# Expert rows weighted at their eviction, and gathers that add into the tokens' rows, in a two-layer Mamba/attention/mixture-of-experts kernel

## Chip, core and metric

The kernel runs on one core of a Trainium2 chip. The metric is the device time of one execution in microseconds (us). Engines are named as in the profile: PE (TensorE), DVE (VectorE), ACT (ScalarE), POOL (GpSimd), SP (SyncE, which here only issues DMAs). Each engine runs its own instructions strictly in order; they meet at semaphores. Indirect DMAs (gather and scatter by a list of row numbers) are issued by POOL and make up the software queue q0; SP's DMAs are q1 and ACT's q10.

## What is computed

Two layers over 8 x 512 tokens of 256 features. Layer 0 adds a bidirectional state-space block and a top-1 mixture of experts. Layer 1 adds attention over a low-rank latent and a top-2 mixture with a capacity. The change touches only that last mixture:

```python
cap = ceil(n_tok / n_exp * 1.0)                     # 4096 / 8 = 512
weights_flat = softmax(x @ router_w.T + router_b)   # [4096, 8]
topk_vals, topk_idx = top_k(weights_flat, 2)        # expert 7 is a no-op
sorted_indices = argsort(-expert_mask, axis=0)[:cap]    # the first 512 tokens of each expert
inputs = x_flat[used_idx] * sorted_mask
h = relu(einsum('ceh,ehi->cei', inputs, experts_inter))
out = einsum('cei,eih->ceh', h, experts_out) * in_w[..., None]
combined = zeros.at[used_idx].add(out)
combined = combined + x_flat * (noop_w * noop_mask)[:, None]
```

Each of seven experts takes the first 512 tokens that chose it; later choices of it are dropped. Choice 8 is a no-op that adds the token's own normalised row times its share. Each token thus gets back at most two expert rows, each times the softmax share of that expert.

## The kernel before

The 4096 tokens are 32 blocks of 128 (`NTILE`), four to a batch of 512. All of layer 1's second half runs under an order written out by hand (`manual_schedule`), so that the order of the Python calls is the order on every engine.

The frame is attention: 128 steps (8 batches x 4 groups of heads x 4 query blocks, loop at L1504 and after), each for four heads. PE makes scores (L1379), DVE evicts them with a clamp (L1384) and multiplies by the decay band taking the row maximum (L1386), ACT takes exponentials (L1394), PE transposes (L1401), ACT evicts these (L1402), PE multiplies by the values (L1410). A step is `now.scores()`, then slots of other work with `fill()`, then the later parts of the two steps before. In a slot, `fill()` takes the next piece of urgent work (projections of the next batch, the output projection `finish`) or, when there is none, of the experts. Only when both are empty does `more()` advance the combine by one turn, so a step has two combine turns once the experts are done.

- **Routing**, `route1` (L1154): softmax `pr` over the experts, the two choices as one-hot masks, ranks by a prefix sum over tokens, slots. `slot1[:, i, k]` is the row of the expert's buffer that holds choice k of the tokens in block i; dropped and no-op choices get row `NSLOT1`. `wsel[k]` holds the shares of choice k (L1201).
- **Send**, `send_rows` (L1286): per block, two scatters on POOL (L1296) send the block's rows to their slots in `xd1` (DRAM), where a row number beyond the buffer is dropped; then DVE adds the no-op part to `x_sb` (L1303), which holds the residual rows of all tokens in SBUF. `ask_rows` loads four blocks ahead. `turn` (L1313) copies the two columns of row numbers of a block to a small tile `at`, of which there are six, since each DMA needs a list of its own.
- **Experts**, `experts` (L1217): for each of seven experts and two halves of 256 slots: load rows (`expert_rows`), transpose, two matmuls with a relu between, evict the result with an ACT copy (L1254), store to `yd1` in DRAM (L1256).
- **Combine**, `combine` (L1337): a turn per block makes two gathers on POOL (L1344) from `yd1` into tiles `yg` of their own, 14 of them; six turns later `add` (L1355) does two weighted adds on DVE (L1358), `x_sb += yg[k] * wsel[k]`. After every fourth block the batch is marked as combined, and if its `finish` has run, `send` (L1333) stores it with SP (L1335). Row `NSLOT1` of `yd1` is zeroed, so dropped choices add zero.
- **Finish** (L1319) of a batch: output projection on PE, eviction on ACT, add to `x_sb` on DVE (L1327).

Of the kernel before, what the change touches and what calls it, by code (L numbers as in the profile page):

```python
# [9 lines left out]
FP = mybir.dt.float32  # L10
# [26 lines left out]
NE1 = NE - 1  # L37
NSLOT1 = NE1 * CAP
HALF = CAP // 2


AH, AD, DL = 16, 16, 64
# [15 lines left out]
def tile_kernel(ctx: ExitStack, tc: tile.TileContext, t, out: bass.AP):  # L58
# [6 lines left out]
    def ctile(name, shape, dtype=FP, pool=None):  # L65
        return (pool or const).tile(shape, dtype, name=name, tag=name)
# [27 lines left out]
    G.iota(iota_t, pattern=[[P, NTILE]], base=0, channel_multiplier=0, allow_small_or_imprecise_dtypes=True)  # L94
    iota_b = ctile("iota_b", [P, NBLK])
    G.iota(iota_b, pattern=[[1, NBLK]], base=0, channel_multiplier=0, allow_small_or_imprecise_dtypes=True)
    zero = ctile("zero", [P, DM])
    G.memset(zero, 0.0)


    xd0 = dram.tile([NBLK * P, DM], FP, name="xd0", tag="xd0")
    yd0 = dram.tile([NBLK * P, DM], FP, name="yd0", tag="yd0")
    xd1 = dram.tile([NSLOT1, DM], FP, name="xd1", tag="xd1")
    yd1 = dram.tile([NSLOT1 + 1, DM], FP, name="yd1", tag="yd1")

    x1 = dram.tile([NT, DM], FP, name="x1", tag="x1")
# [11 lines left out]
    def clear(dst, rows, lo, hi):  # L118

        n = rows // P  # L120
        A.dma_start(
            out=dst[: n * P, :].rearrange("(p r) d -> p r d", p=P)[:, lo:hi, :], in_=bc(zero, 1, [P, hi - lo, DM])
        )


# [353 lines left out]
        Y.dma_start(out=exd.rearrange("g p l -> p g l"), in_=e8)  # L479

    steps()
    l1c = tl = w_r = rb = w_q = w_o = w_uk = w_uv = w_kv = band = slot1 = wsel = proj1 = vt0 = qk0 = r1b = noop = None
    tls = ExitStack()
    for k in range(HC):
        V.tensor_scalar(w_out[:, k, :], w_out[:, k, :], norm_w[:, k : k + 1], None, ALU.mult)
# [1 line left out]
    with ExitStack() as es:  # L487
# [168 lines left out]

        def second_weights():

            nonlocal l1c, tl, w_r, rb, w_q, w_o, w_uk, w_uv, w_kv, band, slot1, wsel, proj1, vt0, qk0
            es.close()  # L660
            l1c = ctx.enter_context(tc.tile_pool(name="l1c", bufs=1, side="right"))
            tl = tls.enter_context(tc.tile_pool(name="tl", bufs=1, side="right"))
            w_r = load("w_r", [P, KC, NE], l1c)
            rb = load("rb", [P, NE], l1c)
            w_q = load("w_q", [P, KC, DM], l1c)
            w_o = load("w_o", [P, KC, DM], l1c)
            w_uk = load("w_uk", [DL, DM], l1c)

            w_uv = ctile("w_uv", [DL + 1, VW], pool=l1c)
            G.memset(w_uv, 0.0)  # L670
            hv = w_uv[:, : AH * (AD + 1)].rearrange("p (h e) -> p h e", e=AD + 1)
            Y.dma_start(out=hv[:DL, :, :AD], in_=t["w_uv"])
            G.memset(hv[DL : DL + 1, :, AD : AD + 1], 1.0)
            slot1 = ctile("slot1", [P, NTILE, 2], I32, l1c)
            wsel = [l1c.tile([P, NTILE], FP, name=f"wsel{k}", tag=f"wsel{k}") for k in range(2)]
            proj1 = ctile("proj1", [P, NTILE, NE], pool=l1c)
            vt0 = ctile("vt0", [P, TPB, VW], pool=l1c)
            qk0 = rows_qk()

            band = ctile("band", [P, NBAND], pool=l1c)  # L680
            G.iota(
                band, pattern=[[1, NBAND]], base=P - S, channel_multiplier=-1, allow_small_or_imprecise_dtypes=True
            )

            w_kv = ctile("w_kv", [P, KC, DL], pool=l1c)
            both = tl.tile([P, 2, KC, DM], FP, name="w_kt", tag="xr", bufs=2)
            Y.dma_start(out=both[:, 0], in_=t["w_kt"])
# [15 lines left out]
            V.tensor_copy(w_kv, wp)  # L703
            yield
# [330 lines left out]
        with tc.manual_schedule(engines=ENGINES):  # L1035
# [39 lines left out]
            for n in range(N):  # L1075
# [43 lines left out]
                if n % 8 == 3 and n // 8 < NE1:  # L1119
                    e = n // 8  # L1120
                    clear(xd1, NSLOT1, TPB * e, TPB * (e + 1))
                    if e == 0:
                        A.dma_start(out=yd1[NSLOT1 : NSLOT1 + 1, :], in_=zero[0:1, :])
            last = batch[B - 1]
            pending.append(last.gate())
            while pending:
# [17 lines left out]
    with tc.tile_pool(name="a1", bufs=1) as p1, tc.tile_pool(name="a2", bufs=2) as p2, tc.tile_pool(  # L1144
# [9 lines left out]
        def route1():  # L1154
# [29 lines left out]


            V.tensor_tensor(noop, pr[:, :, NE1], mask[:, :, NE1], ALU.mult)


            valid = big.tile(E3, FP, name="valid", tag="valid")
# [5 lines left out]
            for k, (m, oh) in enumerate(((m1, oh1), (m2, oh2))):  # L1195
                yield
                V.tensor_tensor(oh, oh, valid, ALU.mult)
                sl = slots_of(big, oh, rank, "k")
                V.tensor_scalar(sl, sl, float(NSLOT1), None, ALU.add)
                V.tensor_copy(slot1[:, :, k], sl)  # L1200
                V.tensor_copy(wsel[k], slots_of(big, oh, pr, "w"))  # L1201

        def expert_rows(e, half):
            at = slice(e * CAP + half * HALF, e * CAP + (half + 1) * HALF)
            xd = e2.tile([P, 2, DM], FP, name="e_xd", tag="e_rows")
            Y.dma_start(out=xd, in_=xd1[at, :].rearrange("(c p) d -> p c d", p=P))
            return xd  # L1210

# [5 lines left out]
        def experts():  # L1217
            w1, xd = expert_w1(0), expert_rows(0, 0)
            yield
            for e in range(NE1):  # L1220
                w2 = e1.tile([P, FC, DM], FP, name="e_w2", tag="e_w2")
                Y.dma_start(out=w2, in_=t["eo"][e])
                for half in range(2):
# [3 lines left out]
                    for k in range(KC):  # L1227
                        for c in range(2):
                            T.transpose(tp[:, k, c * P : (c + 1) * P], xd[:, c, k * P : (k + 1) * P], ident)
                    A.copy(xdT, tp)  # L1230
                    yield
                    hT = e1.tile([P, FC, HALF], FP, name="e_hT", tag="e_hT")
                    for f in range(FC):
# [8 lines left out]
                        xd = expert_rows(e, 1)  # L1242
                    elif e + 1 < NE1:
                        w1, xd = expert_w1(e + 1), expert_rows(e + 1, 0)
                    yo = e2.tile([P, 2, DM], FP, name="e_yo", tag="e_rows")
                    for c in range(2):
                        yp = bank("e_yp", [P, DM])
                        for f in range(FC):
                            T.matmul(  # L1249
                                yp, hT[:, f, c * P : (c + 1) * P], w2[:, f, :], start=(f == 0), stop=(f == FC - 1)  # L1250
                            )
                            if f % 2 == 1 and f < FC - 1:
                                yield True
                        A.copy(yo[:, c, :], yp)  # L1254
                        yield
                    Y.dma_start(out=yd1[at, :].rearrange("(c p) d -> p c d", p=P), in_=yo)  # L1256

        def spread(rows, got, n, by=None):

# [26 lines left out]
        def send_rows():  # L1286

            sent = []
            for i in range(NTILE):
                b, c = i // TPB, i % TPB  # L1290
                if c == 0 and b + 2 < B:
                    ask_rows(b + 2)
                x = to_send[b][:, c, :]
                at = turn(r1b, i)
                for k in range(2):
                    one = G.indirect_dma_start(  # L1296
                        out=xd1, out_offset=bass.IndirectOffsetOnAxis(ap=at[:, k : k + 1], axis=0),
# [5 lines left out]
                V.scalar_tensor_tensor(x_sb[:, i, :], x, noop[:, i : i + 1], x_sb[:, i, :], ALU.mult, ALU.add)  # L1303
                yield

        to_send = {}

        def ask_rows(b):
            to_send[b] = r1b.tile([P, TPB, DM], FP, name="xs", tag="xs", bufs=B)
            Y.dma_start(out=to_send[b], in_=rows_of(xn1, b))  # L1310
            Y.dma_start(out=x_sb[:, b * TPB : (b + 1) * TPB, :], in_=rows_of(x1, b))

        def turn(pool, i):  # L1313

            at = pool.tile([P, 2], I32, name="at", tag="at", bufs=6)
            V.tensor_copy(at, slot1[:, i, :])
            return at

        def finish(b, oT):  # L1319
            for c in range(TPB):  # L1320
# [15 lines left out]

        def combine():  # L1337

            held = []
            for i in range(NTILE):  # L1340
                held.append((i, [e2.tile([P, DM], FP, name="yg1", tag="row1", bufs=14) for _ in range(2)]))
                at = turn(e2, i)
                for k in range(2):
                    G.indirect_dma_start(  # L1344
                        out=held[-1][1][k], out_offset=None, in_=yd1,
                        in_offset=bass.IndirectOffsetOnAxis(ap=at[:, k : k + 1], axis=0),
                        bounds_check=NSLOT1, oob_is_err=False,
                    )
                yield
                if len(held) > 6:  # L1350
                    add(*held.pop(0))
            for one in held:
                add(*one)

        def add(i, yg):  # L1355
            xi = x_sb[:, i, :]
            for k in range(2):
                V.scalar_tensor_tensor(xi, yg[k], wsel[k][:, i : i + 1], xi, ALU.mult, ALU.add)  # L1358
            b = i // TPB
            if i % TPB == TPB - 1:  # L1360
                combined.add(b)
                if b in finished:
                    send(b)

# [282 lines left out]
```

## Time and profile before

| | us |
|---|---|
| Time, median of 3 runs (lowest to highest) | 2100.1 (2098.34 to 2104.96) |
| The profiled execution | 2129.08 |
| Its span | 2127.2 |
| PE, DVE, ACT, POOL busy | 1861.6, 1461.2, 1179.0, 643.6 |
| Index copies of the send, first and last start | 1190.4 and about 1318 |
| Experts' second matmuls, first and last start | 1351.1 and 1965.4 |
| Gathers of the combine, first and last start | 1969.6 and 2091.3 |
| 64 gathers of the combine, POOL time of one (median) | 1.009 |
| 64 weighted adds, DVE time of one (median) | 0.483 |
| 28 evictions of expert rows, ACT time of one (median) | 0.373 |

An execution under the profiler is longer than the runs that are timed; the profile's durations are compared with its own 2129.08 us. In the profile a line of a timeline gives start, duration, engine, source line, operation, output and inputs, and in brackets how long the engine was idle before and what released it. Merged entries (`x2`) give the time from the first start to the last end; DVE instructions overlap[...], so the distance of two starts is what an instruction costs in a full queue. A row of the view by stretch gives, for a window in us from the start, the busy time of each engine with its number of instructions, the clock granted to TensorE (1.00 is full), the busy share of the 16 DMA engines, and GB/s. In a DMA queue's row stand packets, MB and the share of the 16 engines' time in the window.

### The profile page before, as it was taken

What the parts mean: (1) busy time and instruction counts of PE and PEld (TensorE: products, weight loads), DVE (VectorE), ACT (ScalarE), POOL (GpSimd) and SP (SyncE); (2) the same over time, 40 slices, a digit from 0 to 9 for tenths busy, and PEclk for the clock granted to TensorE, in tenths of its full rate; (3) what the DMA queues carried; (4) which work ended last, traced back from release to release, by engine and by line L of the source; (5) the groups of instructions that cost most, each with busy time, mean ns of one, the idle gap of its engine ahead of it and who ended that gap; (6) DMA issues with size and microseconds to landing.
All of it is one profiled execution on the core that took longest, in us unless ns stands there. A gap on an engine that the chain in (4) does not pass through costs nothing. (4 is left out here: it accounts for less than half of the span.)

```text
span 2127.2 us, 33330 instructions
## 1 busy us (share of the span) xinstructions
PE 1861.6 (88%) x11672; PEld 1231.4 (58%) x11672; DVE 1461.2 (69%) x3329; ACT 1179.0 (55%) x2545; POOL 643.6 (30%) x592
## 2 busy tenths in 40 slices
PE   5666999999999999986758788999999999999785
PEld 5333776767677677644535444656666666666443
DVE  5684757575575757687648886666666676767795
ACT  2243544445354544545327566777677777777663
POOL 0048645456464646345400353000000000000552
PEclk9877999999999999997858778999999999999787
DMA  7113745556555556435433342121221212221355
GB/s 259 58 55 128 239 154 190 182 170 208 169 199 181 179 172 193 126 110 158 142 96 110 104 136 76 65 96 61 66 80 62 97 59 87 65 74 56 95 108 95
DMA packets 156632, 263.67 MB, mean 124 GB/s; under 512 B 24906, under 2 KB 113022, under 8 KB 144562
## 3 DMA queue, kind: packets, MB, share of 16 engines
q1 hardware_dynamic: 124816, 144.70, 21.6%
q0 software_dynamic: 22320, 107.55, 16.4%
q10 hardware_dynamic: 9330, 9.31, 1.3%
q8 instruction: 92, 1.51, 0.3%
q14 instruction: 74, 0.61, 0.1%
HBM read 193.44 MB, written 72.75 MB: 125 GB/s over the span
## 5 line engine op out<-in xcount | busy, mean ns | idle before, releaser
L1384 DVE TENSOR_SCALAR s<-s_ps 128x512 f32<-128x512 f32 x512 | 317.8, 683 | 241.6 <-PE s_ps L1379 195.9
L1394 ACT ACTIVATE s<-s,ng 128x512 f32<-128x512 f32 x512 | 354.4, 727 | 32.8 <-DVE ng L1390 23.1
L1401 PE MATMUL p_ps<-ident,s 128*128 128x128 f32 x2048 | 301.5, 292 | 72.4 <-ACT pT L1402 61.6
L1401 PEld LDWEIGHTS p_ps<-ident,s 128*128 128x128 f32 x2048 | 247.6, 149 | 159.7 <-ACT pT L1402 91.4
L1402 ACT COPY pT<-p_ps 128x512 f32<-128x512 f32 x512 | 279.1, 590 | 91.0 <-PE p_ps L1401 63.3
L1386 DVE CUSTOM_DVE_ANT_0 s<-s,band 128x512 f32<-128x512 f32 x512 | 322.8, 688 | 0.0
L1344 POOL DMA_INDIRECT yg<-yd,at x64 | 68.3, 1067 | 705.1 <-ACT s L1394 650.4
L728 PE MATMUL pj<-xT,w_in 128*128 128x512 f32 x384 | 204.5, 660 | 16.0 <-DVE cv L741 14.2
L1379 PE MATMUL s_ps<-kT,qT 16*128 16x512 f32 x1024 | 174.1, 694 | 17.9 <-DVE s L1384 11.5
L541 PEld LDWEIGHTS h_ps<-xdT,w 128*128 128x128 f32 x1248 | 150.1, 193 | 21.0 <-issue 20.2
L541 PE MATMUL h_ps<-xdT,w 128*128 128x128 f32 x1248 | 153.7, 277 | 1.6 <-DMA w<-in_w_dram,w_idx 1.6
L741 DVE SCALAR_TENSOR_TENSOR cv<-pj,w_conv_w,cv 128x511 f32<-128x511 f32 (+2 forms) x192 | 143.1, 746 | 9.6 <-ACT cv L737 5.6
L559 PE MATMUL y_ps<-w,hT 128*128 128x256 f32 x624 | 147.4, 380 | 0.0
L904 POOL TENSOR_TENSOR au<-da,half 128x512 f32<-128x512 f32 x64 | 77.7, 1214 | 212.0 <-PE seg L920 108.1
L1410 PE MATMUL o_ps<-pT,vt 128*32 128x256 f32 x2048 | 139.0, 414 | 0.0
L559 PEld LDWEIGHTS y_ps<-w,hT 128*128 128x128 f32 x624 | 116.0, 191 | 32.1 <-issue 17.9
L728 PEld LDWEIGHTS pj<-xT,w_in 128*128 128x128 f32 x384 | 71.8, 205 | 100.3 <-issue 92.2
L978 POOL TENSOR_TENSOR yT<-yT,ex 128x512 f32<-128x512 f32 (+1 forms) x48 | 59.7, 1243 | 226.3 <-DVE ex L977 168.1
L1236 PE MATMUL e_hp<-e_xdT,e_w 128*128 128x256 f32 x448 | 121.7, 394 | 3.0 <-ACT e_xdT L1230 2.1
L1249 PE MATMUL e_yp<-e_w,e_hT 128*128 128x256 f32 x448 | 120.0, 390 | 0.2
L933 ACT ACTIVATE mt<-seg,mid 64x64 f32<-64x64 f32 x512 | 109.9, 310 | 0.8
L1410 PEld LDWEIGHTS o_ps<-pT,vt 128*32 128x32 f32 x2048 | 64.7, 117 | 77.5 <-issue 48.0
(275 smaller groups left out, 3028.8 us busy)
## 6 DMA issues: line engine op xcount, KB each, us to landing
ex<-exd SPq DMA_DIRECT2D x96, 128.0 KB
u<-in_u_dram SPq DMA_DIRECT2D x16, 512.0 KB
xtd<-xT SPq DMA_DIRECT2D x16, 512.0 KB
fr<-fdd SPq DMA_DIRECT2D x64, 128.0 KB
od<-os SPq DMA_DIRECT2D x32, 256.0 KB
xT<-xtd SPq DMA_DIRECT2D x15, 512.0 KB
e_w<-in_ei_dram SPq DMA_DIRECT2D x7, 1024.0 KB
e_w<-in_eo_dram SPq DMA_DIRECT2D x7, 1024.0 KB
```

The lines of the kernel that those rows point to most:

```text
L541: T.matmul(hp[:, i, :], w1[:, k * FF + f * P : k * FF + (f + 1) * P], xdT[:, k * P : (k + 1) * P], start=(k == 0), stop=(k == KC - 1),)
L559: T.matmul(yp, hT[f // 4][:, f % 4, :], w2[:, f * DM : (f + 1) * DM], start=(f == 0), stop=(f == FC - 1))
L728: T.matmul(pj, w_in[:, k, o * P : (o + 1) * P], self.xT[:, k, :], start=(k == 0), stop=(k == KC - 1))
L741: V.scalar_tensor_tensor(cv[:, s:], pj[:, : S - s], conv_w[:, q, 3 - s : 4 - s], cv[:, s:], ALU.mult, ALU.add)
L1236: T.matmul(hp, w1[:, k, f * P : (f + 1) * P], xdT[:, k, :], start=(k == 0), stop=(k == KC - 1))
L1379: T.matmul(sp[i], self.q[r, cols], self.k[r, :], start=True, stop=True)
L1384: V.tensor_scalar(self.p[i], sp[i], -CLAMP, CLAMP, ALU.max, ALU.min)
L1386: V.tensor_tensor_reduce(out=self.p[i], in0=self.p[i], in1=band[:, at : at + S], scale=1.0, scalar=-3.0e38, op0=ALU.mult, op1=ALU.max, acc ...
L1394: A.activation(self.p[i], self.p[i], AF.Exp, bias=self.ng[:, i : i + 1])
L1401: T.transpose(pp[:, k, :], self.p[i][:, k * P : (k + 1) * P], ident)
L1402: A.copy(pT[i][:, :, cc * P : (cc + 1) * P], pp)
L1410: T.matmul(op[32 * i : 32 * i + 32, half * 2 * P : (half + 1) * 2 * P], self.v[:, k, h * (AD + 1) : h * (AD + 1) + 32], pT[i][:, k, :], st ...
```

## The change

The row that is sent to an expert becomes 264 wide instead of 256: the block's eight shares travel behind its features. When a batch's first block is sent, DVE copies the shares of its four blocks behind the rows. The expert's loads have the wider rows, DVE copies the expert's own column of shares to a tile, and ACT multiplies by it as it evicts. `yd1` then holds weighted rows. The selection of shares in routing goes (`wsel`).

The gathers of the combine write to no tile of their own: they add in the DMA (`compute_op=ALU.add`) to the token's row in `x_sb`. A block's second gather comes three turns after its first, so the loop has 35 turns. Each gather has an index tile of its own (one column is copied), out of the same six. The weighted adds on DVE and their 14 tiles are gone, and a batch's stores are issued once the second gather of its last block has been.

```diff
+DW = DM + NE
-    zero = ctile("zero", [P, DM])
+    zero = ctile("zero", [P, DW])
-    xd1 = dram.tile([NSLOT1, DM], FP, name="xd1", tag="xd1")
+    xd1 = dram.tile([NSLOT1, DW], FP, name="xd1", tag="xd1")
...
+            to_send["shares"] = pr
...
-                V.tensor_copy(wsel[k], slots_of(big, oh, pr, "w"))
...
-            xd = e2.tile([P, 2, DM], FP, name="e_xd", tag="e_rows")
+            xd = e2.tile([P, 2, DW], FP, name="e_xd", tag="e_rows")
...
+                    share = e2.tile([P, 2], FP, name="e_sh", tag="e_sh")
+                    V.tensor_copy(share, xd[:, :, DM + e])
...
-                        A.copy(yo[:, c, :], yp)
+                        A.mul(yo[:, c, :DM], yp, share[:, c : c + 1])
...
+                if c == 0:
+                    V.tensor_copy(to_send[b][:, :, DM:], to_send["shares"][:, i : i + TPB, :])
...
-        def turn(pool, i):
-
+        def turn(pool, i, of):
+
+            of = of if isinstance(of, slice) else slice(of, of + 1)
             at = pool.tile([P, 2], I32, name="at", tag="at", bufs=6)
-            V.tensor_copy(at, slot1[:, i, :])
-            return at
+            V.tensor_copy(at[:, of], slot1[:, i, of])
+            return at[:, of]
...
         def combine():
-            held = []
-            for i in range(NTILE):
-                held.append((i, [e2.tile([P, DM], FP, name="yg1", tag="row1", bufs=14) for _ in range(2)]))
-                at = turn(e2, i)
-                for k in range(2):
-                    G.indirect_dma_start(
-                        out=held[-1][1][k], out_offset=None, in_=yd1,
-                        in_offset=bass.IndirectOffsetOnAxis(ap=at[:, k : k + 1], axis=0),
-                        bounds_check=NSLOT1, oob_is_err=False,
-                    )
+            for i in range(NTILE + 3):
+                for k, j in ((0, i), (1, i - 3)):
+                    if 0 <= j < NTILE:
+                        at = turn(e2, j, k)
+                        G.indirect_dma_start(
+                            out=x_sb[:, j, :], out_offset=None, in_=yd1,
+                            in_offset=bass.IndirectOffsetOnAxis(ap=at, axis=0),
+                            bounds_check=NSLOT1, oob_is_err=True, compute_op=ALU.add,
+                        )
+                b = j // TPB
+                if j >= 0 and j % TPB == TPB - 1:
+                    combined.add(b)
+                    if b in finished:
+                        send(b)
                 yield
-                if len(held) > 6:
-                    add(*held.pop(0))
-            for one in held:
-                add(*one)
-
-        def add(i, yg):
-            xi = x_sb[:, i, :]
-            for k in range(2):
-                V.scalar_tensor_tensor(xi, yg[k], wsel[k][:, i : i + 1], xi, ALU.mult, ALU.add)
-            ...
```

More of the change, by code (lines that the diff above doesn't have):

```diff
@@ L121, in clear @@
         A.dma_start(
-            out=dst[: n * P, :].rearrange("(p r) d -> p r d", p=P)[:, lo:hi, :], in_=bc(zero, 1, [P, hi - lo, DM])
+            out=dst[: n * P, :].rearrange("(p r) d -> p r d", p=P)[:, lo:hi, :],
+            in_=bc(zero[:, : dst.shape[1]], 1, [P, hi - lo, dst.shape[1]]),
         )
@@ L481, in tile_kernel @@
     steps()
-    l1c = tl = w_r = rb = w_q = w_o = w_uk = w_uv = w_kv = band = slot1 = wsel = proj1 = vt0 = qk0 = r1b = noop = None
+    l1c = tl = w_r = rb = w_q = w_o = w_uk = w_uv = w_kv = band = slot1 = proj1 = vt0 = qk0 = r1b = noop = None
     tls = ExitStack()
@@ L657, in second_weights @@
         def second_weights():
-            nonlocal l1c, tl, w_r, rb, w_q, w_o, w_uk, w_uv, w_kv, band, slot1, wsel, proj1, vt0, qk0
+            nonlocal l1c, tl, w_r, rb, w_q, w_o, w_uk, w_uv, w_kv, band, slot1, proj1, vt0, qk0
             es.close()
@@ L674, in second_weights @@
             slot1 = ctile("slot1", [P, NTILE, 2], I32, l1c)
-            wsel = [l1c.tile([P, NTILE], FP, name=f"wsel{k}", tag=f"wsel{k}") for k in range(2)]
             proj1 = ctile("proj1", [P, NTILE, NE], pool=l1c)
@@ L1122, in tile_kernel @@
                     if e == 0:
-                        A.dma_start(out=yd1[NSLOT1 : NSLOT1 + 1, :], in_=zero[0:1, :])
+                        A.dma_start(out=yd1[NSLOT1 : NSLOT1 + 1, :], in_=zero[0:1, :DM])
             last = batch[B - 1]
@@ L1244, in experts @@
                         w1, xd = expert_w1(e + 1), expert_rows(e + 1, 0)
-                    yo = e2.tile([P, 2, DM], FP, name="e_yo", tag="e_rows")
+                    yo = e2.tile([P, 2, DW], FP, name="e_yo", tag="e_rows")
                     for c in range(2):
@@ L1253, in experts @@
                                 yield True
-                        A.copy(yo[:, c, :], yp)
+                        A.mul(yo[:, c, :DM], yp, share[:, c : c + 1])
                         yield
-                    Y.dma_start(out=yd1[at, :].rearrange("(c p) d -> p c d", p=P), in_=yo)
+                    Y.dma_start(out=yd1[at, :].rearrange("(c p) d -> p c d", p=P), in_=yo[:, :, :DM])
         def spread(rows, got, n, by=None):
@@ L1292, in send_rows @@
                     ask_rows(b + 2)
+                if c == 0:
+                    V.tensor_copy(to_send[b][:, :, DM:], to_send["shares"][:, i : i + TPB, :])
                 x = to_send[b][:, c, :]
-                at = turn(r1b, i)
+                at = turn(r1b, i, slice(0, 2))
                 for k in range(2):
@@ L1302, in send_rows @@
                     sent.append(one)
-                V.scalar_tensor_tensor(x_sb[:, i, :], x, noop[:, i : i + 1], x_sb[:, i, :], ALU.mult, ALU.add)
+                V.scalar_tensor_tensor(x_sb[:, i, :], x[:, :DM], noop[:, i : i + 1], x_sb[:, i, :], ALU.mult, ALU.add)
                 yield
@@ L1308, in ask_rows @@
         def ask_rows(b):
-            to_send[b] = r1b.tile([P, TPB, DM], FP, name="xs", tag="xs", bufs=B)
-            Y.dma_start(out=to_send[b], in_=rows_of(xn1, b))
+            to_send[b] = r1b.tile([P, TPB, DW], FP, name="xs", tag="xs", bufs=B)
+            Y.dma_start(out=to_send[b][:, :, :DM], in_=rows_of(xn1, b))
             Y.dma_start(out=x_sb[:, b * TPB : (b + 1) * TPB, :], in_=rows_of(x1, b))
-        def turn(pool, i):
+        def turn(pool, i, of):
+            of = of if isinstance(of, slice) else slice(of, of + 1)
             at = pool.tile([P, 2], I32, name="at", tag="at", bufs=6)
-            V.tensor_copy(at, slot1[:, i, :])
-            return at
+            V.tensor_copy(at[:, of], slot1[:, i, of])
+            return at[:, of]
         def finish(b, oT):
@@ L1337, in combine @@
         def combine():
-            held = []
-            for i in range(NTILE):
-                held.append((i, [e2.tile([P, DM], FP, name="yg1", tag="row1", bufs=14) for _ in range(2)]))
-                at = turn(e2, i)
-                for k in range(2):
-                    G.indirect_dma_start(
-                        out=held[-1][1][k], out_offset=None, in_=yd1,
-                        in_offset=bass.IndirectOffsetOnAxis(ap=at[:, k : k + 1], axis=0),
-                        bounds_check=NSLOT1, oob_is_err=False,
-                    )
-                yield
-                if len(held) > 6:
-                    add(*held.pop(0))
-            for one in held:
-                add(*one)
-        def add(i, yg):
-            xi = x_sb[:, i, :]
-            for k in range(2):
[L1358 to L1363, printed above, removed]
+            for i in range(NTILE + 3):
[12 more added lines that the diff above has]
+                        send(b)
+                yield
         class Step:
```

## The prediction, made before the changed kernel ran

> **What bounds the kernel now.** I read the page's slices first, then busy time by stretch, then the timelines of VectorE (DVE) and GpSimd (POOL) where the change acts, then the DMA queues there. The change touches three stages: routing (about 1137 to 1320 us), experts (1330 to 1968), and combine, the gathers that bring expert rows back (1968 to 2093). The experts' stage is bound by TensorE, the combine by VectorE:
>
> ```profile
> core 0: us, PE busy (x) PEld busy (x) DVE busy (x) ACT busy (x) POOL busy (x), PEclk, DMA share, GB/s
> 1750.00:1850.00 100.00, 96.57 (x719) 62.38 (x717) 69.97 (x180) 75.09 (x147) 0.00 (x0) 1.00 0.24 76
> ...
> 1994.57:2093.00 98.43, 80.66 (x595) 46.53 (x588) 96.90 (x267) 67.23 (x120) 55.61 (x52) 0.88 0.61 122
> ```
>
> While experts run, PE is busy 96.6 of 100 us. From 1994.57 to 2093.00, 14 attention steps with combine turns between them, DVE is busy 96.9 of 98.4 us. One step there, on DVE:
>
> ```profile
> 2057.07 0.17 DVE L1390 TENSOR_SCALAR ng<-mx 128x4 f32<-128x4 f32 x1
> 2057.15 1.00 DVE L1358 SCALAR_TENSOR_TENSOR x_sb<-yg,wsel,x_sb 128x256 f32<-128x256 f32 x2
> 2058.06 0.16 DVE L1316 COPY at<-slot 128x2 int32<-128x2 int32 x1
> 2058.13 1.00 DVE L1358 SCALAR_TENSOR_TENSOR x_sb<-yg,wsel,x_sb 128x256 f32<-128x256 f32 x2
> 2059.05 0.17 DVE L1316 COPY at<-slot 128x2 int32<-128x2 int32 x1
> ```
>
> The score work of the next step starts at 2059.12 with no idle before it, the one after at 2066.13: a step is 7.01 us, of which two pairs of weighted adds take 2 x 0.91 us and two index copies 2 x 0.07. After the last score batch (2093.08) some 34 us remain: exponentials, values, four dependent DMAs, output projection. The 14 adds left over then (2093.0 to 2099.5) lie beside that chain.
>
> **What goes from the combine.** All 64 adds (L1358). 50 of them, 25 pairs, lie before 2093: 25 x 0.915 = 22.9 us from the bounding engine. Index copies become one per gather, so 25 or so more at about 0.07 us: +1.8. DVE's own floor for these 98.4 us is thus 77.3 us. PE comes next: 80.66 us over 14 steps is 5.76 us a step at the granted clock 0.88; packed as in the experts' stage (0.966 busy) about 6.0 us. POOL's four gathers a step are 4 x (1.01 + 0.30) = 5.2 us (the rows below). So where gathers keep up, a step falls from 7.0 to 6.0 us, not to DVE's 5.4.
>
> **What the combine gets: waits on landed gathers.** In the changed program's instruction order, each index copy waits for the landing of the gather six places back, because an index tile now serves one gather instead of two and there are still six. Four gathers a step: a step's last copy waits for the second gather of the step before. Before, the distance was twelve. Queued behind this copy on DVE are the score evictions, and behind those PE and ACT. Cost in the cold case: the second gather starts about 0.43 + 1.31 = 1.74 us after its copies (copy at 2058.06, gathers at 2058.49 and 2059.81), and lands some 2.8 us later, read in the first layer's combine, where the adds did wait:
>
> ```profile
> 1056.96 1.83 POOL L585 DMA_INDIRECT yg<-yd,slot  x1
> 1059.09 1.12 POOL L585 DMA_INDIRECT yg<-yd,slot  x1 [0.30 <-issue]
> ...
> 1060.57 0.48 DVE L610 SCALAR_TENSOR_TENSOR xr<-yg,gate,xr 128x256 f32<-128x256 f32 x1 [0.56 <-DMA yg<-yd,slot]
> ...
> 1062.04 0.48 DVE L610 SCALAR_TENSOR_TENSOR xr<-yg,gate,xr 128x256 f32<-128x256 f32 x1 [0.31 <-DMA yg<-yd,slot]
> ```
>
> 1060.57 and 1062.04 are 1.8 us behind the ends of their gathers' POOL spans; 1.0 + 1.8 = 2.8. So 4.5 us, inside a step of 6.0; the wait costs nothing until a gather takes about 1.5 us more.
>
> It can, because half the gathers are hot. Dropped and empty assignments all point at the zero row of yd1. The scatters show it: in 1190 to 1250 us the software queue moved 3.28 MB, in 1250 to 1320, with as many scatters, 0.41. Counting the reference's routing by block of 128 tokens, from block 19 on all 128 rows of both gathers are that one row. The software queue, three packets on each of 16 engines per gather (48):
>
> ```profile
> q0 software_dynamic: 390, 1.07, 27.5%
> ...
> q0 software_dynamic: 279, 0.75, 70.9%
> ```
>
> The first is 2010 to 2025: 390/48 = 8.1 gathers in 0.275 x 15 us, 0.51 us of all engines each (0.45 in 1968 to 1990). The second is 2060 to 2070: 5.8 gathers in 7.09 us, **1.22 us each**. The trace has no gather that adds. It must read the token's row in SBUF besides the source. Lower bound: nothing more, 1.22. Nearest row: the second read costs what a cold gather costs, 1.22 + 0.45 = 1.67. The Trainium skill speaks against the change here: "Collectives: The Full Stack", the section on the bandwidth ceiling, says that the adder in the DMA path is free but an add needs two source reads on one ring, and halves the rate; that is 2.44 us. By the row a hot step takes 4 x 1.67 = 6.7 us, by the rule 4 x 2.44 = 9.8. I take the row: the slow part is one crowded source row, which the second read does not touch; both ends stay in the range.
>
> A second rule, in "DMA: Bandwidth & Descriptors", rules for kernel authors, demands that an accumulating DMA wait for any earlier one on the same bytes. The program does: a token block's second gather waits on POOL for its first. But seven gathers lie between, 7 x 1.31 = 9.2 us against 2.8 to 4 of landing; by the bare rule a wait of 2.8 us per block, by this order nothing.
>
> **The sum for the combine.** Cold part, 1994.6 to 2043.1 (7 score batches): 48.5 becomes 7 x 6.0 = 42.0, **-6.5**. Hot part, 2043.1 to 2093.0 (7 batches): 49.9 becomes 7 x 6.7 = 46.8, **-3.1**. The burst before 1994 and the 34 us behind 2093 stay. The three extra turns (35 for 32) fall in the last step; three copies go to DVE ahead of the last reciprocal, which has 9.9 us of idle before it. SP gets the output stores three turns sooner, waiting for landings instead of DVE; at most about 3 us ahead of the attention's own DMAs, which have a step of slack. The final adds need the last gathers, which land some 20 us before them.
>
> **Routing.** The two selections of shares go: 1181.65 to 1182.65 and 1189.36 to 1190.36, 2.0 us on a DVE that has no idle there. Eight copies of shares (128x32, about 0.1 us net) come: +0.8. **-1.0** with rounding. Scattered rows are 1056 bytes instead of 1024; POOL's scatter took 0.98 us whether its rows were dropped or not, and the queue was 14% busy, so nothing, at most 3% of the moves.
>
> **Experts.** 28 evictions change from a copy (373 ns) to a multiply by a per-row share: ACT's nearest is the relu of the same shape, 393 ns, so 0.6 us in all on an engine 75% busy; 14 copies of shares on DVE, 0.1 us each at 70%. Both lie beside PE's 97%. Without that cover 2 us. Bounds: -0 to +2; I take 0.
>
> **Forecast.** -6.5 - 3.1 - 1.0 = -10.6 us: the profiled execution (2129.1 us, span 2127.2) becomes 2118.5. The unprofiled median of 2100.1 is 1.4% shorter; the saving carried over whole gives 2089.5, say **2090**.
>
> **Rivals.**
> 1. *The adding gather is twice as long (slower).* Place: the last index copy of each hot step, which waits for a landing, with DVE's score work behind it. Hot part 7 x 9.8 = 68.3, +18.4; with -6.5 and -1.0, +10.9: **2111**. It decides from 2.05 us per hot gather (7 x 8.2 eats the other savings). For it: the rule, and queues 71% busy already. Against: the hot price belongs to the source row.
> 2. *POOL becomes the bound.* Three descriptors a row instead of two: 1.5 + 0.3 = 1.8 us, 7.2 a step, 14 x 7.2 = 100.8 against 98.4, less 1.0: **2102**, no change. Against: 8 KB rows (L506, least 997 ns) and dropped rows cost POOL no more than these.
> 3. *Everything hides.* The clock recovers, gathers cost nothing extra: DVE's floor, 98.4 to 77.3, and -1.0: **2078**.
> That adds are done in two places, or not gone, I exclude: the order of the changed program has none of the 64.
>
> **Chances.** Forecast 0.37; rival 3 0.09; rival 2 0.18; rival 1 0.27; something far worse (each row's add unpipelined) 0.09, beyond the range. Range 2078 to 2120, from rival 3 to rival 1 with a landing delay on top; the forecast's own is 2084 to 2094. A change under 0.3% (6.3 us) can't be told from none. Faster 0.46, same 0.18, slower 0.36.
>
> **What would show it.** The step (distance of score batches) at about 6 us before and 6.7 us after block 19; DVE idle before the index copies near 0 in the cold part, up to 1.3 in the hot; POOL spans of the gathers still 1.0 us; the software queue at about 1.7 us per hot gather. Wrong if a hot gather takes over 2 us or POOL spans grow.

## The result and the profile after

The changed kernel takes **2106.02 us** (median of 15 runs, 2104.08 to 2110.89), the kernel before, run beside it on the same chip, 2102.37 (15 runs, 2094.41 to 2105.85): ratio 1.0024, 95% interval 1.0014 to 1.0033. It is slower by some 3.6 us, within the 0.3% that the prediction called no change, and not faster by 10.6.

One thing must be settled before two traces are laid side by side. In the trace of before, ACT's groups have 28.7 us of idle that end in "remote", a releaser without a name, 19.4 us of it in the send and 9.3 at the first gathers. Another execution of the same kernel (run e0_before below) and the changed kernel's have none there. So the times in this section are compared with e0_before: span 2103.2 us, and 2103.4 for the changed kernel. That the first profile was 29 us above the timed runs belongs to that execution: e0_before's, 2105.19 us, lies among the timed runs of its chip (2094.30 to 2108.46), so a profiled execution is not longer as such.

The view by stretch, over the last 14 attention steps from score batch to score batch, first in the kernel before (columns as in the prediction):

```profile
1964.09:2062.98 98.89, 83.01 (x585) 47.35 (x583) 97.18 (x268) 69.66 (x125) 56.38 (x54) 0.84 0.56 122
```

and in the changed kernel:

```profile
1957.80:2063.44 105.64, 87.25 (x581) 50.90 (x579) 78.36 (x245) 69.88 (x124) 85.26 (x53) 0.79 0.63 117
```

DVE fell from 97.2 busy us to 78.4, as forecast (floor 77.3), and yet the 14 steps take 105.6 us instead of 98.9: 7.55 a step, 7.06 before. The column that rose is POOL's, 56.4 to 85.3, with as many instructions (54 and 53). The answer for the index tile's name shows why: durations as minimum, median and maximum in ns, then first and last start. The kernel before:

```profile
L1344 POOL DMA_INDIRECT yg<-yd,at x64: 1001/1006/1520, 1954.0 to 2066.3; - x64
```

The changed kernel:

```profile
L1351 POOL DMA_INDIRECT x_sb<-yd,at x64: 1566/1575/2045, 1947.6 to 2075.1; - x64
```

A gather that adds holds POOL for **1.575 us** instead of 1.006. With the 0.30 us of issue between two gathers that is 1.88 us, and four of them are 7.5 us: the mean step that was measured. (Single steps take 5.3 to 9.7 us, as a step that runs other work makes no gathers.) POOL's own timeline shows that it sets the pace. In the kernel before it stops after a step's four gathers until DVE has copied the next row numbers:

```profile
1980.62 1.26 POOL L1344 DMA_INDIRECT yg<-yd,at  x1 [0.30 <-issue]
1983.70 1.00 POOL L1344 DMA_INDIRECT yg<-yd,at  x1 [1.81 <-DVE at L1316]
```

In the changed kernel it goes from gather to gather through the 14 steps, with only two stops over 0.31 us (4.30 and 0.83):

```profile
1979.59 1.57 POOL L1351 DMA_INDIRECT x_sb<-yd,at  x1 [0.30 <-issue]
1981.47 1.57 POOL L1351 DMA_INDIRECT x_sb<-yd,at  x1 [0.30 <-issue]
```

From the first gather to the end of the span the changed kernel needs 2103.4 - 1947.6 = 155.8 us, before 2103.2 - 1954.0 = 149.2. The 14 steps (105.64 against 98.89 us) account for all of that 6.6: the stretch behind the last score batch is unchanged (2103.4 - 2063.44 = 40.0, 40.2 before). Up to the first gather the changed kernel's profile is 6.4 us ahead. None of this can be put down to the change: three later runs with the same code up to there have their first gather at 1952.6, 1952.6 and 1955.2.

How POOL's pace reaches DVE is seen in the timeline of the changed kernel on DVE, between two score batches:

```profile
1977.22 0.17 DVE L1388 TENSOR_SCALAR ng<-mx 128x4 f32<-128x4 f32 x1
1977.30 0.15 DVE L1323 COPY at<-slot 128x1 int32<-128x1 int32 x1
1978.20 0.15 DVE L1323 COPY at<-slot 128x1 int32<-128x1 int32 x1 [0.75 <-DMA x_sb<-yd,at]
1979.80 0.15 DVE L1323 COPY at<-slot 128x1 int32<-128x1 int32 x1 [1.45 <-DMA x_sb<-yd,at]
1981.83 0.15 DVE L1323 COPY at<-slot 128x1 int32<-128x1 int32 x1 [1.88 <-DMA x_sb<-yd,at]
1981.91 2.48 DVE L1382 TENSOR_SCALAR s<-s_ps 128x512 f32<-128x512 f32 x4
```

Where two pairs of adds stood, DVE now waits 4.1 us for landings, and the score batch stands behind the fourth index copy. Over the whole combine the index copies wait 22.5 us (16 waits), 22.1 of it in the 14 steps, and 22.9 us of adds had gone: the removed work came back as idle. The granted clock, 0.79 here and 0.84 before, is not the reason: for PE, DVE waited 0.9 us in these steps. The waits of SP's queue in the changed kernel (instruction, what it waited for, us in total, times, longest) show a second road:

```profile
SPq L1342 <- DMA x_sb<-yd,at: 93.4, 25, 15.7
SPq L1342 <- DVE x_sb L1334: 12.1, 4, 5.6
```

L1342 is the store of finished rows. It waits 93.4 us for landings at the head of SP's queue, and the attention's own small DMAs (`od`, `oT`, `sm`) are queued behind. (In e0_before the stores stood there for some 57 us, waiting for DVE.) Last, the DMA queue from 2040 to 2070, where all gathers read the zero row, in the changed kernel:

```profile
q0 software_dynamic: 2165, 1.97, 54.6%
```

A gather now has 144 packets instead of 48, so this is 15.0 gathers in 0.546 x 30 us: 1.09 us of all engines for a hot gather. In e0_before, 2046 to 2076, it was 0.601 x 30 / 14.4 = 1.25. In the cold part it rose from 0.286 x 40 / 24.4 = 0.47 (e0_before, 1966 to 2006) to 0.486 x 40 / 20.3 = 0.96 us (changed kernel, 1960 to 2000). Even in its busiest 10 us (2055 to 2065) the queue takes 68.6% of the engines; that it doesn't bound this kernel is shown by e2.

### The profile page after: what moved, and what is told of

Read it like the earlier page. It is cut to its first block, busy times and chain, and to the rows that moved or that the text cites. A ratio compares the mean times of both kernels' runs of the same rounds, so it can differ in the third digit from the quotient of the medians.

```text
span 2103.4 us, 33297 instructions
## 1 busy us (share of the span) xinstructions
PE 1858.3 (88%) x11672; PEld 1230.9 (59%) x11672; DVE 1437.0 (68%) x3313; ACT 1179.7 (56%) x2545; POOL 675.8 (32%) x592
## 5 line engine op out<-in xcount | busy, mean ns | idle before, releaser
L1399 PE MATMUL p_ps<-ident,s 128*128 128x128 f32 x2048 | 293.1, 287 | 52.5 <-ACT pT L1400 52.4
L1399 PEld LDWEIGHTS p_ps<-ident,s 128*128 128x128 f32 x2048 | 243.2, 146 | 132.9 <-ACT pT L1400 87.8
L1351 POOL DMA_INDIRECT x_sb<-yd,at x64 | 104.1, 1626 | 674.8 <-PE s_ps L1377 649.7
L730 PE MATMUL pj<-xT,w_in 128*128 128x512 f32 x384 | 204.9, 660 | 16.2 <-DVE cv L743 14.3
L1377 PE MATMUL s_ps<-kT,qT 16*128 16x512 f32 x1024 | 173.1, 678 | 18.9 <-DVE s L1382 12.8
L730 PEld LDWEIGHTS pj<-xT,w_in 128*128 128x128 f32 x384 | 72.6, 207 | 101.5 <-issue 93.5
```

The lines of the kernel that those rows point to most:

```text
L730: T.matmul(pj, w_in[:, k, o * P : (o + 1) * P], self.xT[:, k, :], start=(k == 0), stop=(k == KC - 1))
L1377: T.matmul(sp[i], self.q[r, cols], self.k[r, :], start=True, stop=True)
L1399: T.transpose(pp[:, k, :], self.p[i][:, k * P : (k + 1) * P], ident)
```

## Experiments

Theory A: POOL's time for an adding gather is the bound, and reaches the attention through the six index tiles and through the stores on SP. Theory B: the DMA side holds the gathers up (the second read, or the crowded zero row). Runs e0 to e3 ran on one chip, on which before took 2101.8 us, e4 and e6 to e8 on one where it took 2130.0, e9 to e12 where it took 2128.8. Ratios are to the kernel before on the same chip, with 95% intervals. On the last two chips ACT has those nameless waits in all eight profiles, 6.4 us (e7) to 26.1 us (e4). In six of them they all lie in the send, so the time from first gather to end of span is free of them; in e4 18.1 us and in e12 11.4 us lie behind the first gather. The times in us that were expected of e4, e6 and e7 are those of the first chip; on the other two only ratios and stretches can be held against them.

| run | time, us | ratio | first gather to end, us |
|---|---|---|---|
| changed kernel | 2106.02 | 1.0024 (1.0014 to 1.0033) | 155.8 |
| e0_before | 2105.19 (one run) | | 149.2 |
| e1_tiles | 2104.95 | 1.0012 (1.0004 to 1.0021) | 151.4 |
| e2_skip | 2105.28 | 1.0016 (1.0007 to 1.0025) | 152.4 |
| e3_noadd | 2096.25 | 0.9972 (0.9963 to 0.9982) | 144.7 |
| e4_dveadd | 2131.46 | 1.0009 (0.9991 to 1.0027) | 161.8 |
| e6_tiles_late | 2109.09 | 0.9904 (0.9876 to 0.9931) | 138.5 |
| e7_late | 2125.49 | 0.9980 (0.9966 to 0.9995) | 155.5 |
| e8_tiles_late_skip | 2098.14 | 0.9859 (0.9829 to 0.9889) | 131.6 |
| e9_after | 2126.88 | 0.9988 (0.9973 to 1.0003) | 155.5 |
| e10_later | 2108.15 | 0.9902 (0.9881 to 0.9922) | 140.8 |
| e11_later_skip | 2102.29 | 0.9875 (0.9857 to 0.9892) | 131.8 |
| e12_later_noadd | 2119.72 | 0.9964 (0.9948 to 0.9980) | 154.6 |

### e0_before: the kernel before, once more

> The kernel before, unchanged, profiled again. Its first profiled execution took 2129 us against timed runs of 2102, and its trace has about 20 us of ACT waiting for an unnamed queue, 11 of it while the rows are sent and 9 at the first gathers; the changed kernel's trace has none. If these waits belong to that one execution: no such waits and a span near 2100. If they belong to the kernel: a span near 2127 again with the same waits.

It gave the trace used above: no nameless waits on ACT, POOL 1.006 us a gather, DVE as busy as in the first trace.

### e3_noadd: the same gathers without the addition

```diff
-                            bounds_check=NSLOT1, oob_is_err=True, compute_op=ALU.add,
+                            bounds_check=NSLOT1, oob_is_err=True,
```

The tokens' rows are overwritten, so the sum of tokens' and experts' rows is left out; order, tiles and waits of the program stay.

> The changed kernel with its gathers overwriting the rows and not adding to them; leaves out the addition of the residual and of the first choice. Same gathers, same waits, same six index tiles. Theory A: POOL's span falls from 1.57 to 1.01 us, four gathers are 5.2 us a step, DVE's waits nearly go, time about 2090 to 2095 (what was forecast for the change). Theory B: the zero row is read as before, waits stay in the second half, time 2100 or more.

```profile
L1351 POOL DMA_INDIRECT x_sb<-yd,at x64: 1013/1019/1540, 1952.6 to 2066.1; - x64
```

POOL's time is back at 1.019 us. DVE's waits for landings fall from 22.5 to 8.9 us, the last 14 steps take 93.5 us instead of 105.6, and the kernel is some 10 us faster than the changed one (2096.25 against 2106.02 us; 0.9972 of before, against 1.0024). So the addition is what costs, and 0.56 us of it is paid on POOL at every gather. Even so the run gains less than 6 us on the kernel before, where the prediction had 10.6 with this price on POOL: the remaining waits for landings, and 5.4 us of DVE waiting for `sm`, were not in its sum.

### e2_skip: the addition kept, rows of dropped choices not moved at all

```diff
-                            bounds_check=NSLOT1, oob_is_err=True, compute_op=ALU.add,
+                            bounds_check=NSLOT1 - 1, oob_is_err=False, compute_op=ALU.add,
```

> The changed kernel with the bounds set so that row numbers of the zero row are skipped and not read: no crowded row, and half the rows of the gathers move nothing. Theory A: POOL still spends about 1.57 us per gather (its time did not depend on dropped rows in the scatters), so the steps keep 7.5 us and the time is within 4 us of 2106. Theory B: late gathers land sooner, DVE's waits in the second half go, and the time falls by 6 us or more.

In 2040 to 2070 the software queue of this run now does almost nothing (before the edit, 54.6%):

```profile
q0 software_dynamic: 2304, 0.02, 3.9%
```

16 gathers in 0.039 x 30 us are 0.07 us each, and nothing is gained: 1.0016 of before, DVE still waits 20.4 us for landings. POOL's median is 1.575 us as before the edit, rows moved or not, and the last five steps, with next to nothing to move, still take 7.66 us each. Theory B falls as the cause of the missed gain.

### e1_tiles: 24 index tiles instead of six

```diff
-            at = pool.tile([P, 2], I32, name="at", tag="at", bufs=6)
+            at = pool.tile([P, 2], I32, name="at", tag="at", bufs=bufs)
...
-                        at = turn(e2, j, k)
+                        at = turn(e2, j, k, 24)
```

> The changed kernel with 24 index tiles instead of six in the combine. Theory A (POOL's pace: a gather that adds costs POOL 1.57 + 0.30 us, four are 7.5 us a step, and six tiles tie DVE to that pace): DVE's 22.5 us of waits for landings go, steps fall to about 6 us, POOL still goes from gather to gather without a gap and ends at the same distance from its start (about 128 us), behind the steps but ahead of the final adds; time 2090 to 2098. Theory B (the DMA engines bound the gathers, by the crowded zero row and the second read): DVE's waits go too, but POOL now shows gaps while it waits for earlier gathers, the gathers end later, and the time stays above 2100.

Missed: 2104.95 us. DVE's waits for landings are gone, and steps of 5.28 us appear, but the loss turned up on the second road. SP in this run:

```profile
2029.57 11.84 SPq L1342 DMA_DIRECT2D out_dram<-x_sb  x4
2041.51 0.54 SPq L1429 DMA_DIRECT2D oT<-od  x1
2042.10 0.51 SPq L1430 DMA_DIRECT2D sm<-od  x1
```

and DVE:

```profile
2049.75 0.35 DVE L1435 RECIPROCAL sm<-sm 128x32 f32<-128x32 f32 x1 [15.67 <-DMA sm<-od]
```

Four stores take 11.84 us to issue, since each waits for a landing (14.3 us in all); `oT` and `sm` stand behind them, and DVE idles 15.67 us for `sm`, with all later score batches behind that reciprocal. One step takes 21.3 us. In the changed kernel four stores at the same place take 11.79 us too, but DVE's longest wait for `sm` ahead of the tail is 2.6 us (at 2047.52): held at its index copies, DVE comes to that reciprocal later, so the attention runs no further ahead of POOL.

### e7_late and e6_tiles_late: the stores of a batch eight turns later, without and with 24 tiles

```diff
+        put_off = []
         def finish(b, oT):
+            while b == B - 1 and put_off:
+                send(put_off.pop(0)[1])
...
             for i in range(NTILE + 3):
+                while put_off and i >= put_off[0][0] + 8:
+                    send(put_off.pop(0)[1])
...
-                        send(b)
+                        put_off.append((i, b))
```

> The changed kernel with its six index tiles and the stores put off. Theory A2: the index tiles still tie DVE to 7.5 us a step, DVE's waits for landings stay at about 20 us; only the wait of the last od store on SP goes: 2101 to 2105. Rival (the stores are the whole loss): 2088 to 2096 as with both.

> 24 index tiles, and a batch's output stores put off by eight turns (the last ones to the last batch's output projection), so that SP does not wait for landings ahead of the attention's own DMAs. Theory A2 (POOL's pace reaches the attention by two roads, the index tiles on DVE and the stores on SP; with 24 tiles alone it took the second): DVE waits for neither landings nor sm, steps of 5.5 to 6.5 us, POOL ends some 125 us after its first gather beside the last chain, time 2088 to 2096. Rival (the pace of PE and ACT, or the DMA engines, hold the steps anyway): 2100 to 2105 as with 24 tiles alone.

Late stores alone leave the index tiles in place: 155.5 us from the first gather to the end, as in the changed kernel. Each road closed by itself earns little (151.4 and 155.5), both together 138.5 us: the steps fall to between 5.3 and 7.2 us. The roads lie in parallel, one is enough to hold the attention to POOL's pace. The last eight stores (two batches) still kept SP busy for 20 us ahead of the last `od`.

### e8_tiles_late_skip: the same with dropped rows skipped

> 24 index tiles, stores put off, and zero rows skipped. Theory A2: POOL's pace is the same with or without the rows, so within 3 us of the kernel with both edits. Rival (crowded row): 5 us or more below it.

131.6 us from the first gather on, 0.9859 of before: 7 us better than e6 there, 11 by the medians, where skipping alone (e2) had been worth nothing. Where it is gained is seen in e10 and e11.

### e4_dveadd: weighting at the eviction kept, gathers and adds as before

```diff
-                            bounds_check=NSLOT1, oob_is_err=True, compute_op=ALU.add,
+                            bounds_check=NSLOT1, oob_is_err=False,
...
+                V.tensor_tensor(xi, xi, yg[k], ALU.add)
```

The gathers go to 14 tiles of their own again, and DVE adds without a weight.

> Half of the change alone: rows weighted at the experts' eviction by shares sent along, but gathers into tiles of their own as before, and DVE adds them without a weight. Everything ahead of the combine is the changed kernel's. If that half is a gain of about 1 us in the routing and 64 adds at 0.42 instead of 0.48 us: 2098 to 2101. If it costs (evictions, wider rows): 2103 or more, and then the combine's loss is smaller than thought.

1.0009 (0.9991 to 1.0027), POOL 1.006 us a gather: the weighting and the wider rows neither gain nor lose what this run can measure, some 4 us either way. In the steps a gain is seen: four adds at 0.42 us instead of 0.48 bring a step with two turns from 7.0 to 6.77 us. Of the 161.8 us in the table 18.1 are nameless waits on ACT. So the missed gain lies in the gathers, not in this half of the change.

### e9 to e12: the stores twelve turns later

Twelve turns are 24 gathers, as many as there are tiles, so that a store's rows have landed when SP comes to it (in e10 its stores wait 0.4 us for landings). e10 differs from e6 in this number alone, e11 adds the skip of e2, e12 leaves the addition out (the sum of tokens' and experts' rows, as e3); e9 is the changed kernel.

```diff
-                while put_off and i >= put_off[0][0] + 8:
+                while put_off and i >= put_off[0][0] + 12:
```

> The changed kernel again, as the measure for the other runs of this call. All theories: 1.001 to 1.004 times the kernel before, gathers at 1.57 us of POOL, first gather to end of span about 156 us.

> 24 index tiles, and a batch's stores 12 turns later, so that neither VectorE's copies nor SyncE's queue waits for the gathers before the attention ends. Theory A (the gathers' POOL time of 1.88 us is the bound, and reaches the attention only by these two roads): attention steps fall to 5.4 to 6.0 us, the last reciprocal waits no longer for a queue behind stores, POOL runs its gathers without a gap to the end: 64 x 1.88 = 120 us, and with landing, last adds and last stores 129 to 134 us from first gather to end of span against 156; 0.987 to 0.992 of the kernel before. Theory B (DMA engines or the crowded source row hold the gathers up): the same edit brings at most what e1 brought, 151 us, about 1.001.

> As e10, and rows of dropped choices are skipped instead of adding the zero row. Theory A: POOL's time for a gather stays 1.57 us, so within 2 us of e10, at most the last landings come sooner. Theory B: skipping brings 5 us or more beyond e10, since from block 19 on the gathers then move next to nothing.

> As e10, without the addition in the gathers (it leaves out the sum of tokens' rows and expert rows). Theory A: POOL falls to about 1.02 + 0.30 us a gather, 85 us for all, and POOL is done long before the attention, which now sets the end: 120 to 127 us from first gather to end of span, 5 us or more below e10. If the end of e10 was not POOL's but the attention's own, e12 is within 2 us of e10.

e9 repeats 155.5 us from the first gather on; its ratio of 0.9988 (0.9973 to 1.0003) lies below what was expected. So the loss of 0.24% is not repeated on this chip, and no gain is shown either. e10 shows what theory A promised for the steps. Its last 14:

```profile
1977.99:2058.17 80.18, 68.86 (x579) 39.59 (x577) 76.79 (x244) 67.35 (x122) 67.69 (x42) 0.91 0.62 114
```

80.2 us, 5.73 a step, with DVE busy 76.8 of them: DVE is the bound again, at the floor that the prediction had put at 77.3. POOL has only done 42 instructions in that time; its gathers trail the attention. Against 105.1 us for the last 14 steps of e9 this is 25 us, but from the first gather to the end only 14.7 were gained, and e6, with eight turns, had done as well (138.5 us, 0.9904). The rest is lost behind the last score batch, on DVE in e10:

```profile
2085.90 0.35 DVE L1441 RECIPROCAL sm<-sm 128x32 f32<-128x32 f32 x1 [22.43 <-DMA sm<-od]
2095.58 0.69 DVE L1447 TENSOR_TENSOR oT<-oT,rb 128x512 f32<-128x512 f32 x1 [9.32 <-DMA rb<-rd]
2097.99 0.42 DVE L1338 TENSOR_TENSOR x_sb<-x_sb,fo 128x256 f32<-128x256 f32 x1 [1.72 <-ACT fo L1336]
```

and in e11:

```profile
2079.18 0.35 DVE L1441 RECIPROCAL sm<-sm 128x32 f32<-128x32 f32 x1 [16.24 <-DMA sm<-od]
2084.99 0.76 DVE L1447 TENSOR_TENSOR oT<-oT,rb 128x512 f32<-128x512 f32 x1 [5.46 <-DMA rb<-rd]
2089.76 0.42 DVE L1338 TENSOR_TENSOR x_sb<-x_sb,fo 128x256 f32<-128x256 f32 x1 [4.01 <-DMA x_sb<-yd,at]
```

The trailing gathers are all hot, and now lie beside the chain of four dependent DMAs that ends the attention (`od`, `sm`, `rd`, `rb`). The software queue from 2050 to 2085, in e10 and in e11:

```profile
q0 software_dynamic: 2490, 2.28, 77.6%
q0 software_dynamic: 2520, 0.05, 4.2%
```

From e11 to e10 the two waits of that chain go from 16.24 + 5.46 to 22.43 + 9.32 us, and the stretch behind the last score batch from 42.5 to 50.3. The two pairs of runs agree: from the issue of the last `od` to the multiply with `rb` it is 22.8 us in e10 and 20.6 in e6, but 12.8 and 12.6 with skipped rows (e11, e8), and 12.1 in the changed kernel, whose gathers are over by then. The queue's share is not the measure of it, as it was only 49.0% over the same window in e6. So theory A's expectation that skipping would be worth at most 2 us missed: it is worth 5.9 us (2108.15 to 2102.29), and theory B is right about the tail, once the attention no longer waits for POOL. In e11 the last adds wait for landed gathers (4.01 and, after it, 1.4 to 1.5 us each), POOL's own end. There POOL is the bound: 125.8 us from the start of its first gather to the end of its last, and 6.0 us behind that make 131.8. In all nine traces with adding gathers POOL needs 125.5 to 129.2 us for the 64; what the edits change is how much is left behind its last gather, 26.7 us in the changed kernel.

e12 missed and decides nothing. Its gathers are at 1.02 us and 11.4 us of nameless waits lie behind the first of them; two steps take 14.8 and 16.3 us: in the first ACT has two nameless waits of 4.73 and 4.38 us, and from 2035 to 2072 PE was granted a clock of only 0.77 (0.93 in e10's 2035 to 2058), with DVE waiting for PE. Whether e10 without the addition is faster stays open.

**A version that beats both** is e8, at 0.9859 (0.9829 to 0.9889) of before; e11, at 0.9875 (0.9857 to 0.9892), can't be told from it. Both sum the same values as the changed kernel: a skipped row would have added zero. From the first gather on, they need 24 us less than the changed kernel (131.8 against 155.5 in e11 and e9, on the same chip) and 17.6 less than e0_before (149.2), 0.8% of the time. Their medians gain more on the kernel before, 26.5 us (e11) and 31.9 (e8); the excess may be nameless waits on ACT that were longer there. Neither ran on the chip where before takes 2102 us.

## Why the prediction was wrong

- **The step that failed** is "POOL's four gathers a step are 4 x (1.01 + 0.30) = 5.2 us", with its sign to watch, "POOL spans of the gathers still 1.0 us" (it would be wrong if "POOL spans grow", and they grew). An adding gather takes 1.575 us, so four take 7.5 us, above DVE's 7.0 of before. Rival 2 had POOL as the bound, with 1.8 us a gather and 2102 us; the measured 1.88 and 2106.02 are that rival. Its reason, three descriptors a row instead of two, no run shows: what the profile counts, packets, went from 48 to 144. Why an addition costs POOL 0.56 us stays open. Its argument "8 KB rows and dropped rows cost POOL no more than these" was true and beside the point: e2 shows that POOL's time does not depend on whether rows move, and e3 that it depends on the addition alone.
- **Cold part, -6.5.** Seven steps of 7.59 us (1957.80 to 2010.95) instead of 6.0. The estimate "1.74 + 2.8 = 4.5 us inside a step of 6.0" took POOL's half from the trace of before and the landing from another stage; with the second gather starting later by 0.57 us and landings at a median of 4.9 us in this part instead of 2.8, it is over 7. The slack of "about 1.5 us more" that this wait was given was eaten up, most of it before any addition: e0_before's gathers land in 3.9 us in its cold part. So in e3, at the prediction's own price on POOL, DVE still waits 8.9 us.
- **Hot part, -3.1.** Seven steps of 7.50 us instead of 6.7, but not for the reason weighed there. A hot gather's engine time was 1.09 us, below the prediction's "nearest row" of 1.67 and far below the 2.44 of the rule. The rule of the Trainium skill ("Collectives: The Full Stack", the section on the bandwidth ceiling: two source reads halve the rate) fits where rows are cold, 0.47 to 0.96 us, and not where the row itself is crowded, 1.25 to 1.09. Neither price reached the time of this kernel: the step is POOL's in both parts.
- **SP, "at most about 3 us ahead of the attention's own DMAs, which have a step of slack".** The stores wait 93.4 us at the head of the queue. In the changed kernel this costs little more, since DVE is held already (e7, which takes the stores away, has the same 155.5 us); it cost all of what e1 had freed, with single waits of 15.67 us.
- **DVE's floor, 77.3 us**: right, and reached only in e10 (76.8 busy, 5.73 a step), when both roads were closed. That PE would hold a step at 6.0 was too high: there PE is busy 86% of the time, at a granted clock of 0.91.
- **Routing -1.0, experts 0**: consistent with e4's 1.0009; too small to be shown here, as first gathers of the same code lie up to 7.6 us apart.
- **The tail stays**: right for the change (40.2 and 40.0 us), wrong once gathers trail into it (50.3 in e10).
- **The time itself.** 2106.02 us lies in the range of 2078 to 2120, but by rival 2's road, which was given 0.18, and the forecast's direction was wrong.

## What to carry to other kernels

Moving an add from VectorE into a gather does not make it free: here it made POOL's part of the indirect DMA longer (1.006 to 1.575 us), so before such a change compare POOL's gathers per step, at the price of an adding gather, with the step. When a slower engine sits behind small rotating tiles and behind another engine's DMA queue, each of these is enough to hold the fast path to its pace; close all of them in one experiment before judging any. And work that is allowed to trail comes out somewhere: here beside the four dependent DMAs at the end, where skipping rows that add zero, worth nothing before, became worth 6 to 11 us (e10 to e11, e6 to e8).

## What was not expected of the hardware

- An indirect gather of 128 rows of 1 KB took 1.006 us of POOL as a copy and 1.575 us when it adds, the same with nearly all rows skipped (e2, 1.575).
- Its packets went from 48 to 144, skipped rows included (2304 packets for 16 gathers in e2).
- 128 rows that are all one DRAM row took 1.25 us of the engines as a copy, distinct rows 0.47. With the addition it was 1.09 and 0.96. In e10's tail (2050 to 2085) the hot gathers took 0.776 x 35 us / 17.3 = 1.57 us each, in e6's over the same window 0.490 x 35 / 17.4 = 0.99, beside the same chain. What makes up that difference was not tried.
- In the first trace of before ACT waits 28.7 us for something the profile calls remote, in the stages of scatters and first gathers. Such waits (6.4 to 26.1 us) are in all eight traces from the two chips where before takes 2130 and 2129 us, and in none from the chip where it takes 2102. Their cause is open.
